# A GRU stage on one core: column groups of whole tiles, both cells summed where TensorE turns them, scaling on ScalarE

## The chip, the core and the metric

One core of a Trainium2 chip runs one program. The metric is the device time of one execution in microseconds (us); 724.46 us is the median of three runs of the kernel before. The engines of the core run side by side, each in the order of its own program, and wait for each other on semaphores: TensorE (PE in the profile, PEld for its weight loads), VectorE (DVE), ScalarE (ACT), GpSimd (POOL), and SyncE (SP), which issues the large loads.

## What is computed

Four graph layers run one after the other on a graph of 3327 nodes, padded to 3328 = 26 tiles of 128 rows, with 64 features and a 0/1 adjacency matrix. Each adds to x what it makes of a normalized x. The change lies in the third, here with what the 0/1 matrix makes zero left out:

```python
d = jnp.diag(adj); A = adj - jnp.diag(d)
node_support = concatenate([A @ h, 0], 1)
edge_output = gru_cell(node_support, h, w_ih_e, w_hh_e, b_ih_e, b_hh_e)
edge_support = gat(h, A, A, W_gat, a_gat)    # with a 0/1 matrix: the mean of h @ W_gat over the neighbours
node_output = gru_cell(edge_support, h, w_ih_n, w_hh_n, b_ih_n, b_hh_n)
x = x + d[:, None] * edge_output + d[:, None] * node_output

def gru_cell(x, h, ...):     # gates from x @ w_ih.T + b_ih and h @ w_hh.T + b_hh
    r = sigmoid(ir + hr); z = sigmoid(iz + hz)
    n = tanh(inn + r * hn)
    return (1 - z) * n + z * h
```

So both cells end in `n + z * (h - n)`, and their sum is scaled by the diagonal, node by node.

## The kernel before

Layers 1 and 4 (here 0 and 3) are pairwise sums over all node pairs, `hyperbolic_series`; layers 2 and 3 are `plain_decay` and `plain_gat`. The diff touches `plain_gat` alone. Features lie on partitions there: two halves of the nodes are stacked (partitions 0 to 63 are the features of nodes 0 to 1663, partitions 64 to 127 those of the others), so that every array is 128 x 1664. The 1664 columns are cut into C = 4 groups of BK = 416. PSUM is four slots of two banks each; `bank(k)` names one of the eight banks (`banks`, L1821).

- `block(n)` (L1845) adds one tile's neighbours for all four groups into the banks 0 to 3; 26 blocks run to 428 us. `diagonal` and `degrees` take the diagonal out of the degrees.
- `take` (L1942) copies a group's sums to `xh[0]`, `mean` (L1951) makes the neighbours' means in `deg`, `take2` (L1955) copies these to `xh[1]`.
- Then come K = 8 steps, first the four groups of cell 0, then those of cell 1. `products(u)` (L1960) is 8 FP32 matmuls into four banks, `sigmoids` (L1974) both gates on ScalarE, `before_tanh` (L1982) two instructions on VectorE, `tanh` (L1988) one on ScalarE, `state` (L1991) the rest on VectorE: L1996 h - n, L1998 (cell 1 alone) adds what cell 0 left in `oP`, L1999 times z, L2000 the sum into `oP`.
- `last(i)` (L2009) turns `oP` back to rows, four tiles of 128 columns at a time, by transposes on TensorE (`from_pairs`, L1356), and `use` (L2004) multiplies a bank by the diagonal `d2` (L2006) and adds it to X (L2007), both on VectorE. A tile can lie across two groups of 416.
- Layer 3 then starts with L449, the row means of X, on VectorE.

The order is the program's: within a step it is written out by the loop at L2021. For u = 5 it is products, sigmoids, tanh of step 4, before_tanh of step 5, state of step 4; `last(0)` and `last(1)` come after state(6) in u = 7, state(7), `last(2)` and `last(3)` in u = 8.

Of the kernel before, what the change touches and what calls it, by code (L numbers as in the profile page):

```python
# [10 lines left out]
F32 = mybir.dt.float32  # L11
# [3 lines left out]
AF = mybir.ActivationFunctionType  # L15
# [6 lines left out]
P = 128  # L22
T = 26
NP = T * P
D = 64
BK = 416
# [23 lines left out]
def tile_gnn4(ctx: ExitStack, tc: tile.TileContext, x, adjT, att0, b0, w1, bias1, w_gat, a_gat,  # L50
# [4 lines left out]
    V, G, A, PE = nc.vector, nc.gpsimd, nc.scalar, nc.tensor  # L55
# [3 lines left out]
    def room(**kw):  # L59

        return tc.tile_pool(reuse_waits="tile", **kw)

    ident = const.tile([P, P], F32, name="ident")
# [20 lines left out]
    X2 = X.rearrange("p (h t) d -> p h t d", h=2)  # L84
# [5 lines left out]
    diag = const.tile([P, NP], BF, name="diag")  # L90
# [1255 lines left out]
    def from_pairs(psum, src, use, w=None, tiles=range(T // 2), pt=None):  # L1346


        for t0 in tiles[::4]:
            n = min(4, tiles.stop - t0)  # L1350
            if psum is not None:
                pt = psum.tile([P, 4, 2, D], F32, name="pt")
            for k in range(n):
                cs = slice((t0 + k) * P, (t0 + k + 1) * P)
                if w is None:
                    PE.transpose(pt[:, k, :, :], src[:, cs], ident)  # L1356
                else:
                    PE.matmul(pt[:, k, :, :], src[:, cs], w, start=True, stop=True)
            use(t0, n, pt[:, :n, :, :].rearrange("p t h d -> p h t d"))
# [469 lines left out]
    def plain_gat(masks, zo, deg, first, wg, gru, H, parts, banks, last_x, finish, close):  # L1829
# [3 lines left out]


        HP = NP // 2
        C = HP // BK
        C2 = T // 2
        with ExitStack() as st:
            def bank(k):
                return banks[k]  # L1840

            acc = [bank(k)[:, :BK] for k in range(C)]
            order = [o * C2 + k for ks in (range(T // 4), range(T // 4, C2)) for k in ks for o in range(2)]

            def block(n):  # L1845
                b = order[n]
                mask = masks[b // 2][:, b % 2, :]
                for i, w in enumerate([p[:, b % C2, b // C2, :] for p in parts]):
                    for k in range(C):
                        for o in range(2):  # L1850
                            PE.matmul(acc[k][o * D:(o + 1) * D, :], w,  # L1851
                                      mask[:, o * HP + k * BK:o * HP + (k + 1) * BK],
                                      start=n == 0 and i == 0, stop=n == T - 1 and i == 1)

            def diagonal(k, to):

                dg = bank(to)[:, :BK]
                for o in range(2):
                    PE.matmul(dg[o * D:(o + 1) * D, :], ones_bf[:, :D],
                              diag[:, o * HP + k * BK:o * HP + (k + 1) * BK], start=True, stop=True)  # L1860
                return dg

            def degrees(k, to):
                cs = slice(k * BK, (k + 1) * BK)
                V.tensor_sub(deg[:, cs], deg[:, cs], diagonal(k, to))

            block(0)
            last_x(0)
            degrees(0, 6)
            block(1)  # L1870
            last_x(1)
            degrees(1, 7)
# [4 lines left out]
            hP = pers.tile([P, HP], F32, name="hP")  # L1877

            xh = [[pers.tile([P, HP], F32, name=f"xh{g}{o}") for o in range(2)] for g in range(2)]
            oP = H.rearrange("p k o d -> p (k o d)")  # L1880
# [3 lines left out]
            for _ in range(1):  # L1884
                before = st.enter_context(ExitStack())
                tp = before.enter_context(room(name="pgn", bufs=1))
# [11 lines left out]
                def turn(t0, to):  # L1898

                    n = min(4, C2 - t0)  # L1900
                    pt = bank(to)
# [32 lines left out]
                tp = st.enter_context(room(name="pgp", bufs=1))  # L1934

                steps = [(g, k) for g in range(2) for k in range(C)]
                K = len(steps)
                pg, gates, nns = {}, {}, {}  # L1940

                def take(k, on=A):  # L1942
                    cs = slice(k * BK, (k + 1) * BK)
                    for o in range(2):
                        to, src = xh[0][o][:D, cs], acc[k][o * D:(o + 1) * D, :]
                        if on is A:
                            A.activation(to, src, AF.Copy, scale=1.0 / SH)
                        else:
                            V.tensor_scalar(to, src, 1.0 / SH, None, op0=OP.mult)

                def mean(k):  # L1951
                    cs = slice(k * BK, (k + 1) * BK)
                    V.scalar_tensor_tensor(deg[:, cs], acc[k], 1.0 / SH, deg[:, cs], op0=OP.mult, op1=OP.mult)

                def take2(k):  # L1955
                    cs = slice(k * BK, (k + 1) * BK)
                    for o in range(2):
                        A.activation(xh[1][o][:D, cs], deg[o * D:(o + 1) * D, cs], AF.Copy)

                def products(u):  # L1960
                    g, k = steps[u]
                    cs = slice(k * BK, (k + 1) * BK)
                    wx = gru[g][0]
                    pg[u] = pr, pz, ph, pi = [bank((4 + 4 * u + i) % 8)[:, :BK] for i in range(4)]
                    for i, to in enumerate((pr, pz)):
                        for o in range(2):
                            PE.matmul(to[o * D:(o + 1) * D, :], wx[:, i, :], xh[g][o][:, cs], start=True, stop=True)  # L1967
                    for o in range(2):

                        for to, q in ((pi, o), (ph, 1 - o)):  # L1970
                            r = slice(0, D) if to is pi else slice(D, P)
                            PE.matmul(to[q * D:(q + 1) * D, :], wx[r, 2, :], xh[g][q][r, cs], start=True, stop=True)

                def sigmoids(u):  # L1974
                    brz = gru[steps[u][0]][2]
                    gates[u] = []
                    for i in range(2):
                        sg = tp.tile([P, BK], F32, name=f"gate{i}", bufs=2 + i)
                        A.activation(sg, pg[u][i], AF.Sigmoid, bias=brz[:, i:i + 1])
                        gates[u].append(sg)  # L1980

                def before_tanh(u):  # L1982
                    bt = gru[steps[u][0]][1]
                    nn = nns[u] = tp.tile([P, BK], F32, name="nn", bufs=3)
                    V.scalar_tensor_tensor(nn, pg[u][2], bt[:, 5:6], gates[u][0], op0=OP.add, op1=OP.mult)
                    V.tensor_add(nn, nn, pg[u][3])

                def tanh(u):  # L1988
                    A.activation(nns[u], nns[u], AF.Tanh, bias=gru[steps[u][0]][1][:, 2:3])

                def state(u):  # L1991
                    g, k = steps[u]
                    cs = slice(k * BK, (k + 1) * BK)
                    nn = nns[u]
                    o = tp.tile([P, BK], F32, name="o", bufs=1)
                    V.tensor_sub(o, hP[:, cs], nn)  # L1996
                    if g == 1:
                        V.tensor_add(nn, nn, oP[:, cs])  # L1998
                    V.tensor_mul(o, o, gates[u][1])  # L1999
                    V.tensor_add(oP[:, cs], o, nn)  # L2000

                d2 = dcol.rearrange("p (h t) -> p h t", h=2)

                def use(t0, n, src):  # L2004
                    o = tp.tile([P, 2, 4, D], F32, name="x", bufs=2)
                    V.tensor_mul(o[:, :, :n, :], src, d2[:, :, t0:t0 + n, None].to_broadcast([P, 2, n, D]))  # L2006
                    V.tensor_add(X2[:, :, t0:t0 + n, :], X2[:, :, t0:t0 + n, :], o[:, :, :n, :])  # L2007

                def last(i):  # L2009
                    from_pairs(None, oP, use, None, range(4 * i, min(4 * i + 4, C2)),  # L2010
                               banks[4 + i].rearrange("p (t h d) -> p t h d", h=2, d=D))

                for k in (2, 3):
                    mean(k)
# [3 lines left out]
                for k in (0, 1):  # L2018
                    mean(k)
                take(2)  # L2020
                for u in range(K + 2):  # L2021
                    if u < K:
                        products(u)
                        sigmoids(u)
                    if 0 <= u - 1 < K:
                        tanh(u - 1)
                    if u < K:
                        before_tanh(u)
                    if u < C:
                        take2(u)  # L2030
                    if 0 <= u - 1 < K:
                        state(u - 1)
                    for i in {C + 3: (0, 1), C + 4: (2, 3)}.get(u, ()):
                        last(i)

    def load():
        for ts in HALVES:
# [10 lines left out]
    wt, bias, wg, gru = middle_weights()  # L2048
# [89 lines left out]
```

## Time and profile before

| | us |
|---|---|
| three runs | 723.63, 724.46, 726.26 |
| the profiled execution | 726.38 |
| its span, first to last instruction | 724.6 |
| PE busy | 634.0 (88%) |
| DVE busy | 538.8 (74%) |
| ACT busy | 538.2 (74%) |
| POOL busy | 430.0 (59%) |
| last neighbour sum of layer 2 (L1851) starts | 427.8 |
| first instruction of layer 3 (L449) starts | 464.92 |

A row of the timeline has the start in us from the span's first instruction, the duration, the engine, the line, the operation with output and input tiles (buffer numbers left out), their shapes, how many equal instructions the row merges, and in brackets how long the engine was idle before and what it waited for. A row by window has the busy time of each engine in that stretch with its number of instructions in brackets, and then the TensorE clock that was granted (1.00 is full), the share of the DMA engines' time, and GB/s. TensorE's matmuls overlap in the records: the distance from start to start is what one costs.

### The profile page before, as it was taken

To read this page: it belongs to the slowest core of one execution; us is meant where nothing else is said; L and a number is where in the kernel's file an instruction comes from. 1 tells how busy PE (TensorE), PEld (TensorE's weight loads), DVE (VectorE), ACT (ScalarE), POOL (GpSimd) and SP (SyncE) were. 2 spreads that over 40 slices of the span, in tenths; PEclk is the share of its full clock that TensorE was granted. 3 is DMA by queue.
4 is the path that set the end of the run, shared out by engine and by line. 5 is a ranking of instruction groups with operands and counts; after the bars stand their busy time and mean duration, and the time that the engine had idled before them with its cause. 6 is when DMAs were issued, how large, how long until landed. Compare 5 with 4: busy or idle time off the path is not lost.

```text
span 724.6 us, 11975 instructions
## 1 busy us (share of the span) xinstructions
PE 634.0 (88%) x4227; PEld 258.4 (36%) x4227; DVE 538.8 (74%) x991; ACT 538.2 (74%) x700; POOL 430.0 (59%) x327
## 2 busy tenths in 40 slices
PE   0899999999999799989998997159999999999970
PEld 0622233333333243434445642052223433333320
DVE  6867778777777799999745329887667777777756
ACT  2688888888888785687871577158888889888853
POOL 2599999989999301116520000038887888888840
PEclk9999999999999999999999999559999999999985
DMA  3988888898888716389940000202334444443001
GB/s 64 327 258 278 268 273 261 274 281 273 274 252 269 267 41 240 138 286 350 403 188 1 2 1 1 94 18 72 93 95 134 118 119 138 118 118 117 25 2 51
DMA packets 61638, 119.25 MB, mean 165 GB/s; under 512 B 9568, under 2 KB 34048, under 8 KB 61568
## 3 DMA queue, kind: packets, MB, share of 16 engines
q1 hardware_dynamic: 57216, 118.38, 50.7%
q10 hardware_dynamic: 4352, 0.02, 0.3%
q8 instruction: 35, 0.57, 0.3%
q14 instruction: 35, 0.29, 0.1%
HBM read 115.64 MB, written 0.88 MB: 161 GB/s over the span
## 4 chain that ended last, share of the span: by engine, by line
PE 61%; DVE 16%; POOL 7%; issue 6%; DMA 4%; ACT 3%; ACTq 1%; POOLq 0%; DVEq 0%
PE slot L653 16%; PE slot L661 9%; PE slot L632 8%; PE slot L633 7%; PE slot L1552 6%; POOL sig L621 6%; PE slot L1851 5%; DMA adj<-in 4%; PE slot L1566 4%; DVE same L1447 2%; PE slot L1967 1%; DVE mask L1535 1%; DVE sig L643 1%; ACT sig L618 1%; DVE X L1605 1%
## 5 line engine op out<-in xcount | busy, mean ns | idle before, releaser
L643 DVE SCALAR_TENSOR_TENSOR sig<-slot,sig 128x768 f32<-128x768 f32 (+2 forms) x209 | 212.8, 1018 | 108.9 <-POOL sig L621 108.9
L638 ACT ACTIVATE slot<-slot 128x768 f32<-128x768 f32 (+1 forms) x208 | 177.3, 852 | 55.2 <-PE slot L633 55.1
L621 POOL TENSOR_TENSOR sig<-adj,sig 128x768 f32<-128x768 f32 (+1 forms) x104 | 201.1, 1964 | 15.4 <-ACT sig L618 10.9
L618 ACT ACTIVATE sig<-leftB,right 128x768 f32<-128x768 f32 (+1 forms) x208 | 203.2, 977 | 0.1
L621 POOL TENSOR_TENSOR sig<-mask,sig 128x768 f32<-128x768 fp8e4 (+2 forms) x105 | 173.4, 1665 | 41.0 <-ACT sig L618 40.1
L653 PE MATMUL slot<-sig,Xr 128*64 128x384 f32 (+1 forms) x832 | 170.2, 526 | 5.8 <-DVE sig L643 5.4
L632 PE MATMUL slot<-XC,XT 128*128 128x384 f16 (+1 forms) x416 | 142.2, 342 | 2.7 <-ACT sum L671 1.7
L633 PE MATMUL slot<-XF,XE 73*128 73x384 f16 (+1 forms) x416 | 141.3, 340 | 0.0
L661 PE MATMUL slot<-sig,X 128*32 128x384 f32 (+1 forms) x832 | 94.2, 525 | 0.0
L1558 ACT ACTIVATE w<-slot,ebias 128x832 bf16<-128x832 f32 x76 | 69.2, 952 | 25.1 <-PE slot L1552 24.7
L653 PEld LDWEIGHTS slot<-sig,Xr 128*64 128x64 f32 x832 | 49.8, 135 | 87.9 <-issue 60.6
L632 PEld LDWEIGHTS <-XT 128*128 128x128 f16 x416 | 40.6, 98 | 93.8 <-issue 67.4
L1552 PE MATMUL slot<-mask,rest 128*128 128x416 fp8e4 x208 | 53.9, 341 | 5.2 <-ACT adj L1558 2.8
L1552 PE MATMUL slot<-mask,after 128*128 128x416 fp8e4 x208 | 53.4, 339 | 1.1 <-DVE deg L1576 1.1
L633 PEld LDWEIGHTS <-XE 73*128 73x128 f16 x416 | 40.8, 98 | 28.3 <-issue 3.6
L1447 DVE TENSOR_SCALAR_CACHE_REDUCE same<-late 128x832 fp8e4<-128x832 f32 x48 | 48.4, 1009 | 0.0
L436 POOL MEMSET X<- 128x832 f32 x2 | 1.6, 792 | 69.4 <-DVE o L1996 69.4
L219 POOL TENSOR_TENSOR mask<-mask,offdiag 128x128 fp8e4<-128x128 fp8e4 x26 | 14.7, 577 | 47.2 <-PE slot L1552 46.3
L1851 PE MATMUL slot<-mask,own 128*64 128x416 fp8e4 x416 | 39.6, 345 | 2.2 <-DVE deg L1576 2.2
L661 PEld LDWEIGHTS slot<-sig,X 128*32 128x32 f32 x832 | 16.4, 108 | 67.7 <-issue 66.1
L1566 PE MATMUL slot<-w,h 128*64 128x416 bf16 x304 | 34.0, 345 | 0.0
L542 PE MATMUL pt<-ident_h,Xp 128*64 128x128 f16 x32 | 2.6, 313 | 35.5 <-ACT Xp L481 35.5
(322 smaller groups left out, 685.3 us busy)
## 6 DMA issues: line engine op xcount, KB each, us to landing
adj<-in SPq DMA_DIRECT2D x78, 384.0 KB, 4.4
late<-in SPq DMA_DIRECT2D x48, 416.0 KB, 3.2
adj<-in SPq DMA_DIRECT2D x17, 832.0 KB, 7.1
adj<-in SPq DMA_DIRECT2D x27, 512.0 KB, 5.0
ahead<-in SPq DMA_DIRECT2D x14, 832.0 KB, 7.7
ahead<-in SPq DMA_DIRECT2D x16, 416.0 KB, 6.4
own<-in SPq DMA_DIRECT2D x16, 416.0 KB, 4.9
own<-in SPq DMA_DIRECT2D x8, 832.0 KB, 6.8
```

The lines of the kernel that those rows point to most:

```text
L618: A.activation(sig, leftB[c], AF.Sigmoid, bias=right[:, b:b + 1])
L621: G.tensor_tensor(sig[:, os], adj[:, os], sig[:, os], op=OP.mult)
L632: PE.matmul(L[:, o, :c[1] * P], XT[:, rows], XC[c][:, o, :], start=True, stop=False)
L633: PE.matmul(L[:, o, :c[1] * P], XE[:KE, rows], XF[c][:, o, :], start=False, stop=True)
L638: A.activation(L, L, AF.Arctan, scale=PA / SX ** 2)
L643: V.scalar_tensor_tensor(sig[:, os], slot[:, os, :tiles[k][0][1] * P], PC, sig[:, os], op0=OP.add, op1=OP.mult)
L653: PE.matmul(acc[c][o * D:(o + 1) * D, 0, :n], Xr[:, b, :], sigs[k][:, o, :], start=b == 0, stop=b == T - 1)
L661: PE.matmul(acc[c][q:q + 32, 1, :n], X0[:, b - 1 + i, :], w[:, o, :], start=b == 1, stop=b == T - 1, tile_position=(0, q))
L1552: PE.matmul(cnt[o][:, h, :BK], w, cols(k, o, h), start=w is after and steps[k][1] == T - 1, stop=True, skip_group_check=True)
L1558: A.activation(ws[k][:, o, :, :], cnt[o][:, :, :BK], AF.Exp, scale=-LN2, bias=ebias)
L1566: PE.matmul(acc[c][o * D:(o + 1) * D, h, :BK], parts[i][:, b, :], w[:, o, h, :], start=b == T - 1 and i == 0, stop=b == 0 and i == 1)
L1851: PE.matmul(acc[k][o * D:(o + 1) * D, :], w, mask[:, o * HP + k * BK:o * HP + (k + 1) * BK], start=n == 0 and i == 0, stop=n == T - 1 and ...
```

## The change

The four column groups become 512, 384, 384 and 384 columns, which are 4, 3, 3 and 3 whole tiles (`COLS`, `of(k)`), everywhere in `plain_gat`. `state` leaves terms unsummed: for groups 0 and 1 the terms z(h - n) and n of both cells stay in four arrays (`oP`, `xh[0][0]`, `hP`, `deg`); for group 2 cell 0 is summed in `oP`; for group 3 everything is summed on VectorE as before. `turn_back(k)` turns a group to rows by matmuls with the identity as the moving operand, one for each term, accumulated in one bank: 4 tiles of 4 terms, 3 of 4, 3 of 3; group 3 is 3 transposes. `scale(k)` multiplies by the diagonal: on ScalarE, one instruction for each tile and half (8, 6 and 6), for group 3 on VectorE. `use(k)` adds to X on VectorE. `before_tanh` writes n into `xh[0][0]` or `deg` instead of a tile of its own.

```diff
+            COLS = (0, 4), (4, 3), (7, 3), (10, 3)
+            C = len(COLS)
...
-                    nn = nns[u] = tp.tile([P, BK], F32, name="nn", bufs=3)
+                    nn = nns[u] = (xh[0][0], deg)[g][:, of(k)]
...
-                    V.tensor_sub(o, hP[:, cs], nn)
-                    if g == 1:
+                    nn, z = nns[u], gates[u][1]
+                    o, h = (oP, hP)[g][:, cs], hP[:, cs]
+                    V.tensor_sub(o, h, nn)
+                    if g == 1 and k == C - 1:
                         V.tensor_add(nn, nn, oP[:, cs])
-                    V.tensor_mul(o, o, gates[u][1])
-                    V.tensor_add(oP[:, cs], o, nn)
+                    V.tensor_mul(o, o, z)
+                    if g == 0 and k > 1:
+                        V.tensor_add(o, o, nn)
+                    if g == 1 and k == C - 1:
+                        V.tensor_add(oP[:, cs], o, nn)
...
+                def turn_back(k):
+
+                    terms = [oP] if k == C - 1 else [oP, hP, deg] if k > 1 else [oP, xh[0][0], hP, deg]
+                    t0, n = COLS[k]
+                    pt = turned[k] = bank(4 + k)
+                    for t in range(n):
+                        cs = slice((t0 + t) * P, (t0 + t + 1) * P)
+                        for i, src in enumerate(terms):
+                            if len(terms) == 1:
+                                PE.transpose(pt[:, t * P:(t + 1) * P], src[:, cs], ident)
+                            else:
+                                PE.matmul(pt[:, t * P:(t + 1) * P], src[:, cs], ident, start=i == 0,
+                                          stop=i == len(terms) - 1)
...
+                def scale(k):
+                    t0, n = COLS[k]
+                    o = scaled[k] = tp.tile([P, 2, 4, D], F32, name="x", bufs=2)
+                    if k == C - 1:
+                        V.tensor_mul(o[:, :, :n, :], of_bank(k),
+                                     d2[:, :, t0:t0 + n, None].to_broadcast([P, 2, n, D]))
+                        return
+                    for h in range(2):
+                        for t in range(n):
+                            A.activation(o[:, h, t, :], of_bank(k)[:, h, t, :], AF.Copy, scale=d2[:, h, t0 + t:t0 + t + 1])
+
+                def use(k):
+                    t0, n = COLS[k]
+                    V.tensor_add(X2[:, :, t0:t0 + n, :], X2[:, :, t0:t0 + n, :], scaled[k][:, :, :n, :])
...
+                    if u == K - 1:
+                        turn_back(0)
+                    before_tanh(u)
...
+                tanh(K - 1)
+                scale(0)
+                turn_back(1)
+                scale(1)
+                turn_back(2)
+                state(K - 1)
+                use(0)
+                turn_back(3)
+                use(1)
+                scale(2)
+                scale(3)
+                use(2)
+                use(3)
```

More of the change, by code (lines that the diff above doesn't have):

```diff
@@ L1835, in plain_gat @@
         HP = NP // 2
-        C = HP // BK
         C2 = T // 2
+        COLS = (0, 4), (4, 3), (7, 3), (10, 3)
+        C = len(COLS)
         with ExitStack() as st:
@@ L1840, in bank, with of, wide_as @@
                 return banks[k]
-            acc = [bank(k)[:, :BK] for k in range(C)]
+            def of(k, at=0):
+                t, n = COLS[k]
+                return slice(at + t * P, at + (t + n) * P)
+            def wide_as(k, t):
+                return t[:, :COLS[k][1] * P]
+            acc = [wide_as(k, bank(k)) for k in range(C)]
             order = [o * C2 + k for ks in (range(T // 4), range(T // 4, C2)) for k in ks for o in range(2)]
@@ L1851, in block @@
                             PE.matmul(acc[k][o * D:(o + 1) * D, :], w,
-                                      mask[:, o * HP + k * BK:o * HP + (k + 1) * BK],
+                                      mask[:, of(k, o * HP)],
                                       start=n == 0 and i == 0, stop=n == T - 1 and i == 1)
             def diagonal(k, to):
-                dg = bank(to)[:, :BK]
+                dg = wide_as(k, bank(to))
                 for o in range(2):
                     PE.matmul(dg[o * D:(o + 1) * D, :], ones_bf[:, :D],
-                              diag[:, o * HP + k * BK:o * HP + (k + 1) * BK], start=True, stop=True)
+                              diag[:, of(k, o * HP)], start=True, stop=True)
                 return dg
             def degrees(k, to):
-                cs = slice(k * BK, (k + 1) * BK)
+                cs = of(k)
                 V.tensor_sub(deg[:, cs], deg[:, cs], diagonal(k, to))
@@ L1942, in take @@
                 def take(k, on=A):
-                    cs = slice(k * BK, (k + 1) * BK)
+                    cs = of(k)
                     for o in range(2):
@@ L1951, in mean @@
                 def mean(k):
-                    cs = slice(k * BK, (k + 1) * BK)
+                    cs = of(k)
                     V.scalar_tensor_tensor(deg[:, cs], acc[k], 1.0 / SH, deg[:, cs], op0=OP.mult, op1=OP.mult)
                 def take2(k):
-                    cs = slice(k * BK, (k + 1) * BK)
+                    cs = of(k)
                     for o in range(2):
@@ L1961, in products @@
                     g, k = steps[u]
-                    cs = slice(k * BK, (k + 1) * BK)
+                    cs = of(k)
                     wx = gru[g][0]
-                    pg[u] = pr, pz, ph, pi = [bank((4 + 4 * u + i) % 8)[:, :BK] for i in range(4)]
+                    pg[u] = pr, pz, ph, pi = [wide_as(k, bank((4 + 4 * u + i) % 8)) for i in range(4)]
                     for i, to in enumerate((pr, pz)):
@@ L1974, in sigmoids @@
                 def sigmoids(u):
-                    brz = gru[steps[u][0]][2]
+                    g, k = steps[u]
+                    brz = gru[g][2]
                     gates[u] = []
                     for i in range(2):
-                        sg = tp.tile([P, BK], F32, name=f"gate{i}", bufs=2 + i)
+                        sg = wide_as(k, tp.tile([P, 4 * P], F32, name=f"gate{i}", bufs=2 + i))
                         A.activation(sg, pg[u][i], AF.Sigmoid, bias=brz[:, i:i + 1])
@@ L1982, in before_tanh @@
                 def before_tanh(u):
-                    bt = gru[steps[u][0]][1]
-                    nn = nns[u] = tp.tile([P, BK], F32, name="nn", bufs=3)
+                    g, k = steps[u]
+                    bt = gru[g][1]
+                    nn = nns[u] = (xh[0][0], deg)[g][:, of(k)]
                     V.scalar_tensor_tensor(nn, pg[u][2], bt[:, 5:6], gates[u][0], op0=OP.add, op1=OP.mult)
@@ L1992, in state @@
                     g, k = steps[u]
[L1993 to L1996, printed above, removed]
-                    if g == 1:
-                        V.tensor_add(nn, nn, oP[:, cs])
-                    V.tensor_mul(o, o, gates[u][1])
-                    V.tensor_add(oP[:, cs], o, nn)
-                d2 = dcol.rearrange("p (h t) -> p h t", h=2)
[L2004 to L2007, printed above, removed]
@@ L2009, in last @@
-                def last(i):
-                    from_pairs(None, oP, use, None, range(4 * i, min(4 * i + 4, C2)),
-                               banks[4 + i].rearrange("p (t h d) -> p t h d", h=2, d=D))
+                    cs = of(k)
+                    nn, z = nns[u], gates[u][1]
+                    o, h = (oP, hP)[g][:, cs], hP[:, cs]
+                    V.tensor_sub(o, h, nn)
+                    if g == 1 and k == C - 1:
+                        V.tensor_add(nn, nn, oP[:, cs])
+                    V.tensor_mul(o, o, z)
@@ new lines, in state @@
+                    if g == 0 and k > 1:
+                        V.tensor_add(o, o, nn)
+                    if g == 1 and k == C - 1:
+                        V.tensor_add(oP[:, cs], o, nn)
+                d2 = dcol.rearrange("p (h t) -> p h t", h=2)
+                turned, scaled = {}, {}
+                def turn_back(k):
[10 more added lines that the diff above has]
+                                          stop=i == len(terms) - 1)
@@ new lines, in of_bank @@
+                def of_bank(k):
+                    n = COLS[k][1]
+                    return turned[k][:, :n * P].rearrange("p (t h d) -> p h t d", h=2, d=D)
+                def scale(k):
[8 more added lines that the diff above has]
+                            A.activation(o[:, h, t, :], of_bank(k)[:, h, t, :], AF.Copy, scale=d2[:, h, t0 + t:t0 + t + 1])
@@ L2020, in plain_gat @@
                 take(2)
[L2021 to L2025, printed above, removed]
+                for u in range(K):
+                    products(u)
+                    sigmoids(u)
+                    if u:
                         tanh(u - 1)
-                    if u < K:
-                        before_tanh(u)
+                    if u == K - 1:
+                        turn_back(0)
+                    before_tanh(u)
                     if u < C:
                         take2(u)
-                    if 0 <= u - 1 < K:
+                    if u:
                         state(u - 1)
-                    for i in {C + 3: (0, 1), C + 4: (2, 3)}.get(u, ()):
-                        last(i)
+                tanh(K - 1)
[11 more added lines that the diff above has]
+                use(3)
     def load():
```

## The prediction

> **What bounds the kernel now.** I read the page first, then busy time by window, then the timeline and the chain of waits of the stage that the diff touches, and last the rows elsewhere that price its new operations. The page's chain is mostly TensorE in the two pairwise layers, which are untouched; the diff lies between the neighbour sums of layer 2 (last L1851 at 428) and the first instruction of layer 3 (L449). So the windows, cut where TensorE stops being full:
>
> ```profile
> core 0: us, PE busy (x) PEld busy (x) DVE busy (x) ACT busy (x) POOL busy (x), PEclk, DMA share, GB/s
> 428.00:445.40 17.40, 16.91 (x110) 5.20 (x112) 15.20 (x27) 16.15 (x31) 1.36 (x5) 1.00 0.00 1
> 445.40:464.92 19.52, 6.73 (x37) 2.80 (x33) 17.46 (x32) 4.13 (x7) 0.00 (x0) 0.71 0.19 63
> ```
>
> The first 17.4 us are TensorE's (16.91 busy). The next 19.5 are VectorE's (17.46): TensorE is a third busy, its clock averages 0.71, ScalarE is idle. The timeline of that tail:
>
> ```profile
> 449.51 0.64 DVE L1985 SCALAR_TENSOR_TENSOR nn<-slot,gb,gate 128x416 f32<-128x416 f32 x1
> ...
> 452.95 0.64 DVE L1985 SCALAR_TENSOR_TENSOR nn<-slot,gb,gate 128x416 f32<-128x416 f32 x1
> ...
> 455.88 0.59 DVE L2000 TENSOR_TENSOR own<-o,nn 128x416 f32<-128x416 f32 x1
> 456.39 0.68 DVE L2006 TENSOR_TENSOR x<-slot,dcol 128x512 f32<-128x512 f32 x1
> 457.13 1.33 PE L1356 MATMUL slot<-ident,own 128*128 128x128 f32 x5 [3.71 <-DVE x L2006]
> 459.61 0.58 DVE L1996 TENSOR_TENSOR o<-hP,nn 128x416 f32<-128x416 f32 x1
> 462.00 0.90 PE L1356 MATMUL slot<-ident,own 128*128 128x128 f32 x3 [3.55 <-DVE own L2000]
> 464.60 0.29 DVE L2007 TENSOR_TENSOR X<-X,x 128x128 f32<-128x128 f32 x1
> 464.92 1.94 DVE L449 TENSOR_REDUCE mean<-X 128x13 f32<-128x832 f32 x2
> ```
>
> A step of the second cell costs VectorE 3.44 us (449.51 to 452.95), the turning starts only at 456, and the last state waits behind it. One detail decides much below: the transposes at 457.13 had their operand at 456.47 (end of L2000), but began when L2006 had *read* the other bank of the same two-bank slot (457.07). Waits on PSUM hold for a whole slot. The built program of the changed kernel has the same kind of waits.
>
> **The change, part by part.** Times are on the profile's clock.
>
> *Column groups 512, 384, 384, 384.* The sums stream as many columns as before. TensorE's products start a step every 2.41 us (L1967 at 441.29, 443.70, 446.11); by width that is 2.22 for 384 and 2.97 for 512. Step 1 starts at 431.67 as now (the wider first group lengthens step 0, the narrower take(3) on VectorE returns it); six steps of 2.22 and one of 2.97 end the products at 448.0 (now 448.6). Gain 0.6 at most, or nothing if VectorE were late; it is not:
>
> *VectorE's cells.* Rows: 0.59 for 416 columns, 0.69 for 512, so 0.555 for 384; a next instruction starts after 0.61 if dependent, 0.51 if not (447.26, 447.88, 448.39), so 0.58 and 0.475 at 384. Removed: L2000 for groups 0 and 1 of cell 0 and 0 to 2 of cell 1, L1998 for the latter: 8 instructions. ScalarE keeps its order and sets the pace until the gate of step 4 (about 442.3). From there: 1.39 (before_tanh 4, 512) + 1.64 (state 3) + 1.12 + 1.33 + 1.12 + 1.06 + 1.12 = 8.8, so the last before_tanh ends at 451.1 (now 454.2), its tanh at 451.75, state(7) at 454.4 (now 461.95). VectorE's 7.5 us are won, but they end no chain: what is late next is the turning.
>
> *Turning on TensorE.* 13 transposes become 16 + 12 + 9 = 37 FP32 matmuls plus 3 transposes. The row is L1358, the same 128x128 FP32 shape, two records per matmul:
>
> ```profile
> 326.89 0.83 PE L1358 MATMUL slot<-wt,Xr 128*128 128x128 f32 x6
> 484.97 2.02 PE L570 MATMUL junk<-ident,left 128*128 128x128 f32 x8
> ```
>
> At full clock (0.83 - 0.275)/5 = 0.111 per record; at clock 0.50 (second row) (2.02 - 0.52)/7 = 0.214. A matmul is 0.223 or 0.43, a transpose 0.109 (L1903). The Trainium skill, "TensorE: Matmul & The Clock Gate", section Terms, calls the transpose mode 4 times faster for FP32, which speaks against this change: 37 x 0.436 = 16.1 us. The row says 2 times, 37 x 0.223 = 8.3 us. I take the row. That the terms accumulate in one bank is not in it; L1851 accumulates 52 times into a bank and starts its pairs 0.174 apart at 416 columns, no slower per column than others, so I add nothing (bounds 0 and 0.02 a record, 1.5 us for all 74).
>
> *Scaling on ScalarE.* 20 instructions of 128x64 replace three wide multiplies. Nearest row, same operation and per-partition scale, from SBUF:
>
> ```profile
> 711.98 5.36 ACT L911 ACTIVATE M<-M,am 128x64 f32<-128x64 f32 x22 [5.20 <-DVE am L849]
> ```
>
> (5.36 - 0.332)/21 = 0.24 each. From PSUM the row L1905 (0.278 for 128 columns) suggests 0.22. Bounds 0.20 and 0.333 (no overlap); I take 0.24. ScalarE idles there now, so nothing is queued behind except layer 3's square, far later.
>
> *The new chain.* In TensorE's order turn_back(0) follows the products; it needs state(4)'s multiply (447.84).
> - turn_back(0): 448.2, 32 records, ends 451.9. scale(0): 8 x 0.24 + 0.09, ends 454.0.
> - turn_back(1) writes the other bank of the slot that scale(0) reads, so it waits: 454.1, 24 records, 457.0. turn_back(2), 18 records: 459.0. turn_back(3), 3 transposes: 459.3. VectorE's state(7) (454.4) is long done.
> - scale(2) must wait for turn_back(3), which wrote its slot last: 459.4 to 460.9. VectorE's multiply for group 3 waits for scale(2), then two additions: 0.07 + 0.475 + 0.475 + 0.555, so L449 starts at 462.5.
> Against 464.92 that is -2.4 us at full clock throughout. use(0) and use(1) (0.69, 0.555) fall into VectorE's idle time; if not, they would cost 1.2.
>
> *Other queues.* Layer 3's early loads on SP wait for turn_back(2) instead of a subtraction at 459.6: the same time. GpSimd's fill of Xe moves from 441.7 to about 459 and is wanted after 478. Cost 0, covered by these 19 us; uncovered 0.7.
>
> *The clock.* While scale(0) runs, TensorE is idle 2.2 us. The skill's rule (same page, section "HAM oscillation — how this bites in real kernels") is that gaps above about 3.4 us lose the clock, so the sum would stay -2.4. The trace has a stricter case:
>
> ```profile
> 383.87 1.25 PE L1851 MATMUL slot<-mask,own 128*64 128x416 fp8e4 x12 [2.24 <-DVE deg L1576]
> ```
>
> and by window:
>
> ```profile
> 381.95:385.36 3.41, 1.49 (x14) 1.01 (x14) 1.83 (x4) 0.11 (x1) 0.00 (x0) 1.00 0.02 5
> 385.36:388.77 3.41, 3.41 (x20) 2.27 (x20) 1.18 (x2) 0.00 (x0) 0.00 (x0) 0.50 0.00 0
> ```
>
> After an idle 2.24 us the clock fell to 0.50 at 385.36 and came back 3.41 us later; the other changes (453.63, 487.76, 702.80) lie on the same 3.41 us grid. Counting the columns that the records stream (an FP32 record twice), windows below 0.38 busy lost the clock and those above 0.44 kept it. A window around the new gap has (3.41 - 2.3)/3.41 = 0.33 if it holds all of it, so whether it falls depends on the grid's phase, about one execution in two. A lost window costs 3.41 x (1 - 0.111/0.214) = 1.6 us, leaving -0.8.
>
> **The forecast and the rivals.** The profiled execution took 726.38 (span 724.6, 1.8 around it); the sum is -0.8 to -2.4 on it, and I apply it to the median, 724.46.
> - *Likeliest (0.45)*: some executions lose one window, others none; median -1.6, 722.9, own range 721.5 to 724.
> - *Rival 1, clock kept in every execution (0.25)*: 722.1; with scales of 0.20 (-0.6), 721.5. For it: the gap is under two thirds of a window. Against: the row at 385.
> - *Rival 2, the clock falls in scale(0)'s gap and stays low to the end (0.15)*: 42 records x 0.103 + 3 transposes x 0.1 = +4.6, so +2.2: 726.7, slower than before. It decides when the window after the fall is less busy than the clock needs to return (windows at 0.71 did not bring it back, at 0.96 did). Against: the turning is 0.9 busy.
> - *Rival 3, the change doesn't overlap what it says (0.10)*: the column scales, read from PSUM, run end to end at 0.333; 14 on the chain x 0.094 = +1.3: 724.2 with the median clock.
> - The rest (0.05): a wait that I don't see.
>
> So faster by over 0.5% (3.6 us, about what a measurement here can tell from none) 0.08: it needs everything at its lower bound and the runs' spread of 2.6 us on its side. Slower by over 0.5%: 0.12, rival 2 with rival 3, or the clock gone already in turn_back(0) (+3.3). Within: 0.80. Range: low -2.4 - 0.6 - 1.0 (the spread) = 720.5; high rival 2 with scales of 0.28 (+0.6) = 727.2.
>
> **What would show it.** Right: the last before_tanh near 451 and state(7) near 454, not 462; products ending at 448; 0.111 per record in turn_back(0); a TensorE wait of 2 us on ScalarE's scales; VectorE waiting over 4 us before its last multiply; L449 about 34.5 us after the last L1851 (now 36.9). A clock of 0.50 in turn_back(1) marks the lost window. Wrong: scales above 0.3, records above 0.15 at full clock, steps before 445 that lengthen, or a difference outside this stage.

## The result and the profile after

| | before | changed |
|---|---|---|
| median of 20 runs each, us | 724.11 | 722.63 |
| lowest and highest, us | 722.64, 726.26 | 719.70, 726.15 |
| ratio of the changed kernel to before, 95% interval | | 0.9978 (0.9966 to 0.9991) |
| profiled execution, us | 726.38 | 726.15 |
| PE, DVE, ACT busy, us | 634.0, 538.8, 538.2 | 639.9, 532.1, 542.3 |

The change wins 0.22%, 1.6 us of 724 (0.65 to 2.5 by the interval). The forecast was 1.6 us.

The two profiled executions can't be compared by their spans; the changed kernel's is the slowest of its twenty. The first take of layer 2 starts at 427.86 in the kernel before and at 429.75 in the changed one, though the first two layers are the same code and the sums stream the same columns; over the ten profiled executions of this study with the new column groups it starts anywhere from 425.56 to 432.58. So I compare the stage alone: T is the time from the first take (the first ACTIVATE that copies sums to `xh`) to L449. It was 37.06 before (427.86 to 464.92) and is 36.02 now (429.75 to 465.77). The first takes, before and changed:

```profile
427.86 2.11 ACT L1947 ACTIVATE xh<-slot 64x416 f32<-64x416 f32 x4 [1.18 <-PE slot L1851]
429.75 2.21 ACT L1955 ACTIVATE xh<-slot 64x512 f32<-64x512 f32 x4 [1.20 <-PE slot L1859]
```

The prediction cut the stage at 445.40, 17.54 us after the take. The changed kernel, cut at the same distance from its own take:

```profile
core 0: us, PE busy (x) PEld busy (x) DVE busy (x) ACT busy (x) POOL busy (x), PEclk, DMA share, GB/s
429.75:447.29 17.54, 17.18 (x112) 5.04 (x112) 14.96 (x27) 16.51 (x31) 0.79 (x1) 1.00 0.00 1
447.29:465.77 18.48, 13.71 (x101) 11.13 (x101) 11.34 (x23) 8.36 (x27) 0.55 (x4) 0.91 0.12 39
```

Before, the second stretch had 17.46 us of VectorE in 19.52. Now VectorE has 11.34 in 18.48, TensorE 13.71 and ScalarE 8.36: VectorE no longer sets the end, and nothing is full in its place. The timeline of its end tells who waits:

```profile
452.51 0.55 DVE L1996 TENSOR_TENSOR deg<-deg,slot 128x384 f32<-128x384 f32 x1
...
454.13 1.75 ACT L2047 ACTIVATE x<-slot,dcol 128x64 f32<-128x64 f32 x8 [0.42 <-PE slot L2031]
...
455.69 0.56 DVE L2015 TENSOR_TENSOR own<-hP,deg 128x384 f32<-128x384 f32 x1
...
455.93 0.49 PE L2031 MATMUL slot<-ident,own 128*128 128x128 f32 x2 [1.83 <-ACT x L2047]
...
460.23 1.33 ACT L2047 ACTIVATE x<-slot,dcol 128x64 f32<-128x64 f32 x6 [4.36 <-PE slot L2031]
...
462.88 1.33 ACT L2047 ACTIVATE x<-slot,dcol 128x64 f32<-128x64 f32 x6 [1.31 <-PE slot L2029]
...
464.24 0.56 DVE L2042 TENSOR_TENSOR x<-slot,dcol 128x384 f32<-128x384 f32 x1 [2.08 <-ACT x L2047]
...
465.77 1.95 DVE L449 TENSOR_REDUCE mean<-X 128x13 f32<-128x832 f32 x2
```

The whole cell is over at 456.25 (the end of L2015), 9.5 us before L449. The end hangs on one chain, its waits in the brackets: ScalarE's eight scales wait for turn_back(0); TensorE stands for 1.83 us until they have read the slot (455.93) and then turns the other three groups without a stop, to 462.84; scale(2) waits for turn_back(3); and VectorE, idle, waits 2.08 us for scale(2) before its last multiply. ScalarE's own 4.36 us of waiting for turn_back(1) lie beside TensorE's work and add nothing to the chain.

By window, on the clock's grid:

```profile
core 0: us, PE busy (x) PEld busy (x) DVE busy (x) ACT busy (x) POOL busy (x), PEclk, DMA share, GB/s
453.88:457.29 3.41, 1.58 (x14) 1.39 (x14) 2.90 (x6) 1.75 (x8) 0.00 (x0) 1.00 0.00 0
457.29:460.70 3.41, 3.41 (x19) 3.41 (x18) 0.00 (x0) 0.47 (x3) 0.00 (x0) 0.50 0.00 0
```

The 1.83 us of waiting lie wholly in the first window, TensorE is busy for 1.58 of 3.41 there, and the next window runs at 0.50. This execution is one that lost a window.

### The profile page after: what moved, and what is told of

The parts are those of the page before. It is cut to its first block, busy times and chain, and to the rows that moved or that the text cites. A ratio compares the mean times of both kernels' runs of the same rounds, so it can differ in the third digit from the quotient of the medians.

```text
span 724.4 us, 12112 instructions
## 1 busy us (share of the span) xinstructions
PE 639.9 (88%) x4291; PEld 262.8 (36%) x4291; DVE 532.1 (73%) x980; ACT 542.3 (75%) x720; POOL 433.4 (60%) x327
## 4 chain that ended last, share of the span: by engine, by line
PE 65%; DVE 13%; issue 6%; POOL 5%; DMA 4%; ACT 3%; SPq 2%; ACTq 1%; POOLq 0%; DVEq 0%
PE slot L653 18%; PE slot L661 10%; PE slot L632 9%; PE slot L633 8%; PE slot L1552 6%; PE slot L1859 5%; POOL sig L621 5%; PE slot L1566 4%; DMA adj<-in 3%; DVE same L1447 2%; PE slot L1975 2%; PE slot L2031 1%; DVE mask L1535 1%; ACT sig L618 1%; PE slot L1980 1%
## 5 line engine op out<-in xcount | busy, mean ns | idle before, releaser
L653 PE MATMUL slot<-sig,Xr 128*64 128x384 f32 (+1 forms) x832 | 171.3, 530 | 7.0 <-DVE sig L643 6.9
L661 PE MATMUL slot<-sig,X 128*32 128x384 f32 (+1 forms) x832 | 95.7, 532 | 0.0
L653 PEld LDWEIGHTS slot<-sig,Xr 128*64 128x64 f32 x832 | 50.2, 136 | 88.4 <-issue 63.7
L219 POOL TENSOR_TENSOR mask<-mask,offdiag 128x128 fp8e4<-128x128 fp8e4 x26 | 17.5, 682 | 43.9 <-PE slot L1552 43.8
L1859 PE MATMUL slot<-mask,own 128*64 128x384 fp8e4 (+1 forms) x416 | 39.8, 346 | 2.2 <-DVE deg L1576 2.2
```

Source lines behind the costliest of these rows:

```text
L653: PE.matmul(acc[c][o * D:(o + 1) * D, 0, :n], Xr[:, b, :], sigs[k][:, o, :], start=b == 0, stop=b == T - 1)
L661: PE.matmul(acc[c][q:q + 32, 1, :n], X0[:, b - 1 + i, :], w[:, o, :], start=b == 1, stop=b == T - 1, tile_position=(0, q))
L1859: PE.matmul(acc[k][o * D:(o + 1) * D, :], w, mask[:, of(k, o * HP)], start=n == 0 and i == 0, stop=n == T - 1 and i == 1)
```

## The experiments

The theory at the start: the end of the stage is the chain of slot waits that the prediction wrote down; VectorE's saved sums are not in it; the lost window comes from the gap in it. The rivals: the column groups bring the gain; TensorE's additions bring it; ScalarE's scales are the price. All ratios are to the kernel before, with 95% intervals; T is from each kernel's own profiled execution. The kernels were timed in groups, each beside the kernel before, whose median was 724.11 beside the changed kernel, 724.41 beside e1 to e4, 725.18 beside e5 and e7, and 725.28 beside e8. So ratios can be compared, and medians of different groups can't.

| kernel | T, us | lost window in the turning | median us (runs) | ratio |
|---|---|---|---|---|
| before | 37.06 | | 724.11 (20) | 1 |
| changed | 36.02 | one | 722.63 (20) | 0.9978 (0.9966 to 0.9991) |
| e1_banks | 31.51 | none | 720.94 (6) | 0.9939 (0.9915 to 0.9962) |
| e2_columns | 36.20 | | 724.13 (14) | 1.0001 (0.9985 to 1.0017) |
| e3_sums_on_dve | 34.70 | | 722.53 (11) | 0.9964 (0.9945 to 0.9983) |
| e4_scales_on_dve | 32.44 | none | 721.32 (13) | 0.9947 (0.9931 to 0.9963) |
| after_look2 | 34.40 | none | 727.21 (1) | |
| after_look3 | 34.41 | none | 723.41 (1) | |
| e5_filled | 34.40 | none | 722.64 (13) | 0.9965 (0.9949 to 0.9981) |
| e7_three_terms | 30.70 | none | 719.30 (6) | 0.9924 (0.9908 to 0.9940) |
| e8_banks_and_dve | 31.06 | none | 718.16 (6) | 0.9907 (0.9888 to 0.9926) |

(An empty cell for the window: in the kernel before, e2 and e3 TensorE is idle for most of the tail, and the granted clock is 0.50 from 453.63, 449.61 and 451.00 on to past L449. For after_look2 and after_look3, one run each, no ratio is given.)

**e2: the column groups alone**, in the kernel before.

```diff
+            COLS = (0, 4), (4, 3), (7, 3), (10, 3)
+            C = len(COLS)
...
-                    from_pairs(None, oP, use, None, range(4 * i, min(4 * i + 4, C2)),
+                    from_pairs(None, oP, use, None, range(COLS[i][0], sum(COLS[i])),
```

> The kernel before with the column groups of whole tiles alone (512, 384, 384, 384); sums, transposes and scaling stay as they were. Theory: VectorE's instructions number and stream the same, so its tail stays: within 0.5 us of the kernel before (ratio 0.999 to 1.001), 37 us from the first take to layer 3's first instruction. Rival (whole tiles alone bring the gain, since a tile no longer waits for two groups): about 1.5 us under the kernel before, ratio 0.998.

T is 36.20, where 37 was expected: 0.9 less than before, in one execution each. The runs show no difference (1.0001, and their interval would hold 0.9 us as well). Groups of whole tiles let turn_back take a group by itself; by themselves they are no gain that these runs can measure.

**e3: both cells summed on VectorE**, everything else as changed. TensorE then only transposes.

```diff
-                    if g == 1 and k == C - 1:
+                    if g == 1:
                         V.tensor_add(nn, nn, oP[:, cs])
                     V.tensor_mul(o, o, z)
-                    if g == 0 and k > 1:
-                        V.tensor_add(o, o, nn)
-                    if g == 1 and k == C - 1:
-                        V.tensor_add(oP[:, cs], o, nn)
+                    V.tensor_add(oP[:, cs], o, nn)
...
-                    terms = [oP] if k == C - 1 else [oP, hP, deg] if k > 1 else [oP, xh[0][0], hP, deg]
+                    terms = [oP]
```

> The changed kernel with the addition taken back to VectorE: every state sums both cells, and each group is turned by transposes of the one sum; scaling stays on ScalarE. Theory: the last before_tanh ends about where it did before (454 on the profile's clock, 451 plus the shift of the run in the changed one) and state(7) 2.3 us after state(6), but the turning shrinks from 8.3 us to 1.4, so the two cancel: within 0.7 us of the changed kernel, 1 to 2 us under the kernel before (ratio 0.9975 to 0.9985), 35 us from the first take. Rival (TensorE's additions are where the gain comes from): back to the kernel before or above, ratio 1.000 or more.

T is 34.70, where 35 was expected. The timeline of e3:

```profile
453.15 0.61 ACT L1999 ACTIVATE deg<-deg,gb 128x384 f32<-128x384 f32 x1 [2.62 <-DVE deg L1996]
...
455.46 1.54 PE L2026 MATMUL slot<-ident,own 128*128 128x128 f32 x6 [5.92 <-ACT x L2044]
...
461.25 1.95 DVE L449 TENSOR_REDUCE mean<-X 128x13 f32<-128x832 f32 x2
```

The last tanh starts 26.60 us after the take (453.15 less 426.55), where the changed kernel has it at 23.35: the eight sums are back on VectorE and cost 3.25 us there. Yet T is 34.70 against 34.40 in the executions of the changed kernel that kept the clock (below), and the ratio is 0.9964 against 0.9978, with intervals that overlap. What VectorE wins by giving its sums away, TensorE spends on turning four terms for one. TensorE's additions, the part of the change with the largest diff, are worth 0.3 us of T in this order of banks, and nothing that the runs show; with the banks of e1 it was not tried. From e2 to e3 T falls by 1.5. In e2 VectorE scales and adds groups 0 and 1 ahead of the last state, which ends 33.6 us after the take; in e3 ScalarE scales, VectorE adds behind the state, and it ends at 30.8. Of these 2.7 us, 1.2 go again in the scales behind it. No run parts ScalarE's scaling from that order.

**after_look2, after_look3: the changed kernel again**, to see the clock in other executions.

> The changed kernel itself, looked at once more for the phase of the clock's grid. Theory: a window of 3.41 us at half clock falls on the turning in about one execution in two; from the first take to layer 3's first instruction it is 36.0 us where the clock shows one, and 34.4 where it shows none. Rival (the clock has no part in it): 36.0 in every profile.

> As the look before it: 36.0 us from the first take with a lost window in the turning, 34.4 without one.

The timeline of after_look3:

```profile
454.98 0.49 PE L2031 MATMUL slot<-ident,own 128*128 128x128 f32 x2 [1.84 <-ACT x L2047]
...
463.20 1.95 DVE L449 TENSOR_REDUCE mean<-X 128x13 f32<-128x832 f32 x2
```

T is 34.40 and 34.41: the same to 0.01 us, and 1.6 below the first execution's 36.02. (after_look2 took 727.21 all the same: its stage began only at 432.58.) By window in after_look2:

```profile
core 0: us, PE busy (x) PEld busy (x) DVE busy (x) ACT busy (x) POOL busy (x), PEclk, DMA share, GB/s
456.96:460.37 3.41, 1.60 (x14) 1.60 (x15) 2.67 (x6) 1.75 (x8) 0.00 (x0) 1.00 0.00 0
460.37:463.78 3.41, 3.41 (x33) 3.41 (x32) 0.56 (x1) 1.34 (x6) 0.00 (x0) 1.00 0.00 0
```

Here too the whole gap lies in one window, with 1.60 us busy, and the clock stays at 1.00; in the first execution 1.58 lost it. In after_look3 the grid cuts the gap in two (at 453.75). So this gap stands just at the edge. Counted by the columns that the records stream, as in the prediction, the window that lost had 0.37 and the one that kept 0.42.

**e5: the gap filled.** Eight matmuls without use between scale(0) and turn_back(1), into a bank that nobody reads.

```diff
                 scale(0)
+                for i in range(8):
+                    PE.matmul(bank(0)[:, :P], oP[:, :P], ident, start=i == 0, stop=i == 7)
                 turn_back(1)
```

> The changed kernel with TensorE's gap filled: between turn_back(0) and turn_back(1) it issues 8 FP32 matmuls of the identity into a bank that nobody reads, 16 records of 0.111 us, 1.8 us, while scale(0) runs. Theory (the idle gap is what loses the clock): no half-clock window in the turning in any execution, 34.4 to 34.7 us from the first take, and about 0.7 us under the changed kernel's median, ratio to before 0.997. Rival (the clock falls by chance, or for the number of matmuls): windows at half clock as before, and the median unchanged or up to 1.8 us above it.

The timeline of e5:

```profile
453.78 0.49 PE L2031 MATMUL slot<-ident,own 128*128 128x128 f32 x2
...
461.99 1.95 DVE L449 TENSOR_REDUCE mean<-X 128x13 f32<-128x832 f32 x2
```

turn_back(1) starts 26.19 us after the take (453.78 less 427.59), as in after_look3 and the first execution (26.19, 26.18): filling a wait doesn't shorten it. T is 34.40 with no window lost. That fits the gap as the cause: the five profiled executions without it or with a shorter one (e1, e4, e5, e7, e8) lost no window in the turning, of the three with it one did. With so few it is not proof. The runs' ratio is 0.9965 against the changed kernel's 0.9978, and the intervals overlap, so that filling helps the median is not shown; a loss of 1.6 us in a third of the executions would be 0.0007.

**e1: the slot wait taken away.** turn_back(1) goes into a bank of the other slot.

```diff
-                    pt = turned[k] = bank(4 + k)
+                    pt = turned[k] = bank((4, 6, 5, 7)[k])
```

> The changed kernel with one number list changed: the groups are turned into banks 4, 6, 5, 7 instead of 4, 5, 6, 7, so that turn_back(1) no longer writes the slot that scale(0) reads. Theory (the chain is turn_back(0), scale(0), turn_back(1), turn_back(2), turn_back(3), scale(2), last additions, held together by waits for whole slots): TensorE loses its idle 1.9 us, scale(2) no longer waits for turn_back(3) and the last multiply no longer for scale(2), together 2.8 us at full clock, and no window of the clock is lost (0.8 on average): about 3.5 us under the changed kernel, 5 under the kernel before (ratio 0.993), and from the first take to layer 3's first instruction 31.5 us (36.0 in the changed kernel's profile, 37.1 before). Rival (VectorE's shorter steps made the gain and the turning's waits are covered by it): no difference from the changed kernel, ratio 0.998.

The timeline of e1:

```profile
455.61 1.75 ACT L2047 ACTIVATE x<-slot,dcol 128x64 f32<-128x64 f32 x8 [0.41 <-PE slot L2031]
...
458.29 1.34 ACT L2047 ACTIVATE x<-slot,dcol 128x64 f32<-128x64 f32 x6 [0.93 <-PE slot L2031]
...
460.30 1.34 ACT L2047 ACTIVATE x<-slot,dcol 128x64 f32<-128x64 f32 x6 [0.67 <-PE slot L2031]
...
462.73 1.95 DVE L449 TENSOR_REDUCE mean<-X 128x13 f32<-128x832 f32 x2
```

T is 31.51, where 31.5 was expected, and the ratio's interval lies wholly below the changed kernel's. scale(1) starts 0.93 us after scale(0) is done, not 4.36 (3.03 in after_look3, where the clock was kept), since turn_back(1) ran beside scale(0); and no gap is left to lose a window. One tuple of four numbers is worth 2.9 us against the changed kernel with its clock kept: as much as the whole change (37.06 - 34.40 = 2.7). It takes three waits away. scale(2) starts 29.08 us after the take instead of 31.51 in after_look3: some 2.0 of that is TensorE's stand before turn_back(1), the rest that it no longer waits for turn_back(3). The last 0.5 is the multiply for group 3, which starts at 460.62, beside scale(2) and no longer behind it.

**e4: the scales back on VectorE**, as wide multiplies, scale(0) ahead of state(7) and scale(1) behind it.

```diff
-                    if k == C - 1:
+                    if True:
                         V.tensor_mul(o[:, :, :n, :], of_bank(k),
...
-                scale(1)
-                turn_back(2)
                 state(K - 1)
                 use(0)
-                turn_back(3)
+                scale(1)
+                turn_back(2)
                 use(1)
+                turn_back(3)
                 scale(2)
```

> The changed kernel with ScalarE's scaling undone: all four groups are multiplied by the diagonal on VectorE in one instruction each, group 0 ahead of state(7), group 1 after it. Theory (the 1.75 us of eight 128x64 scales stand in the chain between turn_back(0) and turn_back(1)): scale(0) takes 0.7, TensorE's gap falls to about 0.9 us, too short to lose a window of the clock, and the last scale is 0.56 instead of 1.33: about 1.7 us at full clock and 0.8 of clock under the changed kernel, ratio to before 0.9945, 33 us from the first take. Rival (VectorE is the bound, and ScalarE took work off it): 1.5 us or more above the changed kernel, ratio 1.000.

The timeline of e4:

```profile
452.40 0.69 DVE L2042 TENSOR_TENSOR x<-slot,dcol 128x512 f32<-128x512 f32 x1
...
453.14 0.49 PE L2031 MATMUL slot<-ident,own 128*128 128x128 f32 x2 [0.78 <-DVE x L2042]
...
460.45 1.95 DVE L449 TENSOR_REDUCE mean<-X 128x13 f32<-128x832 f32 x2
```

One multiply of 0.69 us frees the slot, where eight scales took 1.75, and TensorE waits 0.78 instead of 1.83. T is 32.44, somewhat better than expected. Since TensorE took the sums, VectorE has the time for all scaling, and moving it to ScalarE costs 2.0 us of T as the change stands. That is no contradiction to the gain from e2 to e3, where VectorE still has the sums to make.

**e8: e1 and e4 together.** Do the two add up, or do they pay for the same wait?

> The bank order of e1 and the wide VectorE multiplies of e4 together. T is the time from the first take to L449. Theory (what narrow scales on ScalarE cost in the changed kernel is paid at the wait for the shared slot, where TensorE stands behind scale(0) and scale(1); only a little of it is the last scale on the chain): with the waits gone by the bank order, the multiplies on VectorE have little left to win. From the trace of e1: turn_back(2) ends about 460.1 there, 28.9 after the take; the wide scale(2) 0.56 and scale(3) 0.47 after it, then two additions 1.05: L449 at T 30.9, which is 0.6 under e1 instead of the 2.0 that e4 won over the changed kernel. Ratio to the kernel before 0.9925. Rival (the two edits save different things and add up, 2.0 + 2.9): T about 29.5, ratio 0.9905.

The timeline of e8:

```profile
457.63 1.95 DVE L449 TENSOR_REDUCE mean<-X 128x13 f32<-128x832 f32 x2
```

T is 31.06, where 30.9 was expected and 29.5 if they added up: 0.45 less than e1, not 2.0. So nearly all that ScalarE's narrow scales cost was paid at the slot waits. The runs give 0.9907, the fastest version of the study; by T alone it would be (724.1 - 6.0) / 724.1 = 0.992, inside the interval. Its advantage over e7, which was timed in another group, is not shown.

**e7: e1 with three terms.** Cell 0 summed on VectorE for all groups, so that TensorE turns three terms at most, and scale(0) ahead of the last tanh on ScalarE; four buffers for the scaled groups.

```diff
-                    if g == 0 and k > 1:
+                    if g == 0:
                         V.tensor_add(o, o, nn)
...
-                    terms = [oP] if k == C - 1 else [oP, hP, deg] if k > 1 else [oP, xh[0][0], hP, deg]
+                    terms = [oP] if k == C - 1 else [oP, hP, deg]
...
-                tanh(K - 1)
                 scale(0)
+                tanh(K - 1)
```

> The kernel with banks 4, 6, 5, 7, and further: cell 0 is summed on VectorE for all groups, so that groups 0 and 1 are turned from three terms instead of four (14 records fewer on TensorE), scale(0) stands ahead of the last tanh on ScalarE, and the scaled tiles have four buffers. Theory (TensorE's records are the chain, VectorE has room in cell 0 where ScalarE sets the pace): 1.6 us under the kernel with changed banks alone, 29.9 us from the first take (31.5 there), ratio to before 0.991. Rival (VectorE's two additions and the later tanh and state(7) take over): 31.5 us or more from the first take, ratio 0.994 or above.

T is 30.70, the shortest, but 0.8 above what was expected. The timeline of e7:

```profile
451.61 0.55 DVE L1996 TENSOR_TENSOR deg<-deg,slot 128x384 f32<-128x384 f32 x1
...
453.27 0.66 ACT L1999 ACTIVATE deg<-deg,gb 128x384 f32<-128x384 f32 x1
...
453.97 0.56 DVE L2008 TENSOR_TENSOR hP<-hP,deg 128x384 f32<-128x384 f32 x1 [0.74 <-ACT deg L1999]
```

The last tanh had its operand at 452.16 but stood behind scale(0) on ScalarE until 453.27. VectorE waited 0.74 us for it and then worked without a pause up to L449, so this wait is about what T has over 29.9. The expected 29.9 had not counted that queue; the rival had named it, at a higher price.

## Why the prediction was right, point by point

- **Size.** Forecast 1.6 us, measured 1.6 (0.65 to 2.5). That they agree to the tenth is luck: the interval is wider than what parts the likeliest case from rival 1 (2.4 us), two terms below were off in opposite directions, and the share of executions that lose a window was not known.
- **VectorE's saved sums end no chain.** Right: e3 gives them back and loses 0.3 us of T and nothing in the runs. The last before_tanh ends 23.3 us after the take (forecast 451.1 less 427.86, 23.2), state(7) 26.5 (forecast 26.5).
- **Column groups, gain 0.6 at most.** turn_back(0) starts 20.50 us after the take (forecast 448.2, so 20.3). The 0.2 were lost at the start: the prediction let step 1 begin as before (431.67, 3.81 us after the take), and it begins at 433.88, 4.13 after it, so the narrower take(3) does not return what the wider first group costs. Alone they measure as nothing (e2).
- **Turning at 2 records of 0.111 us.** Right: the 32 records of turn_back(0) take from 450.25 to 454.09. Sixteen matmuls of 0.436, an estimate from the rule that was weighed (the Trainium skill, "TensorE: Matmul & The Clock Gate", section Terms), would be 7.0. A matmul at half clock took 0.43 (457.43 and on), as forecast.
- **Scales of 0.24 us.** The term that was mis-sized: eight take 1.75 us and six 1.335, so one is 0.207. It was near the lower bound. On the chain that is 14 x 0.033 = 0.46 us less, of which the start of the turning takes 0.2 back: with the clock kept the stage is 34.40, where the forecast's times make 34.6.
- **The slot wait before turn_back(1), and scale(2) behind turn_back(3).** Right in place; the wait was 1.83 us instead of 2.2, because of the scale. VectorE's wait of over 4 us before its last multiply came in two pieces, 4.75 us before use(1), which needs scale(1), and the 2.08 above; the prediction had not written that use(1) lies between.
- **The clock.** The mechanism was right: an idle stretch of 1.83 us, far below the 3.4 us that the skill's rule ("TensorE: Matmul & The Clock Gate", section "HAM oscillation — how this bites in real kernels") asks for, lost a window of 3.41 us, and it cost 36.02 - 34.40 = 1.62 us (forecast 1.6). "About one execution in two" rested on a window 0.33 busy; with the shorter gap it is 0.37 to 0.42, on both sides of the edge, and one in three lost it. So the likeliest case and rival 1 are nearly the same case, and the runs can't part them.
- **Rival 2** (the clock stays low): in no profile. **Rival 3** (scales end to end at 0.333): refuted by 0.207.
- **What the prediction did not ask.** It took the slot wait as given. e1 shows that the waits for the shared slot were the largest single price in the change, 2.9 us together, and that an order of banks removes them.

So the gain went like this, in T with the clock kept: 0.9 from the columns (one execution each, not seen in the runs), 1.5 from ScalarE's scaling and the earlier last state, 0.3 from TensorE's additions, if they are put in in this order; 37.06 to 34.40. A lost window takes back 1.6 of these 2.7 in some executions.

What stays open: why the unchanged code ahead of the stage ends up to 7 us apart from execution to execution. Most of it arises in layer 0. The four executions that have a window at half clock starting between 148.9 and 150.1 (the three of the changed kernel and e1) are the four whose first take starts latest, at 428.79 to 432.58; the other seven, the kernel before among them, lie between 425.56 and 428.01. In the changed kernel's first execution TensorE stands for 2.02 us at 149.61 before eight matmuls of L653, which then take 2.40 us; in the kernel before it stands for 0.31 at 148.14, and they take 1.51. e8 stands for 2.07 there and keeps its clock. What makes TensorE wait there in some executions and not in others was not followed further, nor whether the changed kernel meets it more often than the others.

## What to carry to other kernels

Before work is moved off the busiest engine, write the chain behind it to the end: here the next engine's waits for a shared PSUM slot were worth more than the sums that were moved. Consecutive stages that hand banks back and forth should alternate slots, not banks, and while others wait for the slot, one wide instruction that frees it can beat several narrow ones, even on the busier engine (2.0 us of T here, and 0.45 once nobody waits). Compare a stage by its own start and end when the code ahead of it varies more than the change is worth.

## What was not expected of the hardware

The clock's edge could be seen from both sides in this stage: of two executions of one kernel with the same 1.83 us gap wholly inside one 3.41 us window, that with 1.58 us of TensorE in the window lost the clock for the next one, that with 1.60 us kept it (0.37 and 0.42 by streamed columns). Busy time alone doesn't tell: with other shapes, in layer 0, the window from 145.52 in e1 lost the clock with 1.75 us of TensorE, and the one from 34.57 in e3 kept it with 1.50. And a narrow ScalarE instruction (128x64 from PSUM, with a scale per partition) cost 0.207 us in a row, less than the same operation from SBUF in the row at 711.98 (0.24).
